# Top-1 mixture of experts after a resampler attention: w2 per turn, shared tiles for the small row groups, five hidden buffers

## The chip, the core and the metric

The kernel runs on one core of one Trainium2 chip. All data is float32. The metric is the device time of one execution in microseconds; the time of a kernel is the median of its runs. TensorE (PE in the profile) multiplies, VectorE (DVE) and ScalarE (ACT) compute elementwise, GpSimd (POOL) computes a little and issues indirect DMAs, SyncE (SP) issues the other DMAs. Each engine runs its instructions in the order in which they are written.

## What is computed

Two stages over 16 sequences of 128 tokens, 256 wide. The first is a resampler attention with 16 heads of 64 and a residual; the change does not touch it. The second is a layer norm and a feed-forward layer with one shared expert and 8 routed experts, of which each token takes one:

```python
scores_aE = x_aD @ router_DE
vals_aK, idx_aK = jax.lax.top_k(scores_aE, 1)
masked_aE = jnp.full_like(scores_aE, -jnp.inf).at[jnp.arange(a)[:, None], idx_aK].set(vals_aK)
gates_Ea = jax.nn.sigmoid(masked_aE).T
routed_in_EaD = gates_Ea[:, :, None] * x_aD[None, :, :]
mid_EaF = silu(einsum('ead,edf->eaf', routed_in_EaD, w1_eDF)) * einsum('ead,edf->eaf', routed_in_EaD, w3_eDF)
routed_out_EaD = einsum('eaf,efd->ead', mid_EaF, w2_eFD)
shared_aD = silu(x_aD @ ws1_DF) * (x_aD @ ws3_DF) @ ws2_FD
out_aD = shared_aD + routed_out_EaD.sum(axis=0)
```

There are 2048 tokens, D = 256, F = 704, 8 experts. The layer adds its result to its input.

## The kernel before

The order of the instructions on all five engines is written out by hand (`manual_schedule`). The attention runs first, eight pairs of sequences after one another, with chunks of the shared expert (`shared_unit`) put between. When its memory is released, at about 520 us, the second stage has the rest of the span.

**Routing** (`route`, L997). Each token has a place among those of its expert. The experts are sorted by their number of tokens, and expert number w in that order gets window w, of 320, 288, 288, 288, 256, 256, 256 and 256 slots (`WINDOWS`). The first 256 slots of window w are tiles 2w and 2w + 1 of 128 rows. What a window has beyond 256, its `REST` (64, 32, 32, 32), is a small tile with the number 16 + w. The number of the slot is worked out by DVE from `win` (the window) and `place` with some twenty small operations (L1098 to L1121, `beyond` at L1106), then `slot_table` (L954) turns it into a table with the token of each slot, with sixteen products `slots` on TensorE (L983). Chunks of the shared expert are put between these by a generator (`yield`). A branch at the end (`overflow`) handles experts that outgrow their window; it is not taken here.

**Weights.** `load_experts` (L920) loads w2 of all 8 experts, in the experts' own order, into one tile `wds`, from the moment that the attention's memory is free. `load_up` (L1236) loads w1 and w3 of one window's expert into one of three tiles `w13`; the first three are issued when the order of the experts is known, and that of window w + 2 in window w. All are issued by SP.

**Inputs.** `gather` (L1188) fetches a tile's rows of `h_rows` by the table, with an indirect DMA of POOL; `gate` (L1201) multiplies them by the gates on DVE. For window 0 TensorE transposes them (`transpose_inputs`, L1207) and DVE copies them to `inputs_t`. For later windows DVE transposes blocks of 32 (`turn_inputs`, L1214), SP writes them to DRAM, and `fetch_inputs` (L1228) reads them back in the right place. `inputs_t` has two tiles, taken in turns.

**Windows.** `up` (L1243) computes chunk f of the hidden layer: four products (two for the half chunk f = 5) on TensorE into a pair of PSUM banks of `ps_s` (two pairs, taken in turns), silu on ACT, the product `mid` on DVE. `out_rows` (L1276) multiplies a tile of `mid`, six products, by w2 into a PSUM bank of `ps_m` (three, in turns), DVE adds the rows of the residual and the shared expert (`sg`, gathered by `stream_rows`, L1264), and POOL scatters the sum to `out`. The expert's number addresses `wds` from a register of TensorE (`value_load`, L1320). A float32 product is two records of the trace. The loop (L1319) goes over the windows:

```python
        for f in range(NF):
            up(w13s[w % 3], inputs_t[w % 2], WINDOWS[w], mids[w % 2], f, f"w{w}")
            if f == 0:
                sgs = [stream_rows(t, rows_of(t)) for t in tiles_of(w - 1)] if w else []
```

After chunk 0 of window w come, in this order: the gathers of `sg` for window w - 1, `turn_inputs(w + 1)`, the gathers for window w + 2, `down_window(w - 1)` with its two or three tiles, `fetch_inputs(w + 1)` and `load_up` for window w + 2. Then chunks 1 to 5. So TensorE's order is chunk 0 of window w, the tiles yr of window w - 1, chunks 1 to 5 of window w. There are two `mids`. `sg` has three buffers (the tag `xr`), gathered rows three (`xg`).

## Time and profile before

| | us |
|---|---|
| median of 3 runs | 748.63 (748.04 to 748.77) |
| profiled execution | 748.45 |
| its span, first to last instruction | 746.6 |
| TensorE busy | 736.0 |
| yr of one window with a small tile, windows 0 to 3 | 8.05 to 8.08 |
| yr of one window without, windows 4 to 7 | 5.34 |
| first products of the experts (chunk 0 of window 0) | from 584.11 |
| first yr tile | from 603.32 |
| SP's loads of w2 issued | 522.88 to 538.4 |
| SP's first loads of w1 and w3 issued | from 542.30 |

The page gives the share of time in which each engine was busy, the same in 40 slices, and the chain of work that ended last, followed back from the last instruction. The timeline lists instructions in the order of time: start, length, engine, line of the code, operation, output and inputs, and in brackets how long the engine stood idle before and what it waited for. A DMA that POOL issues is shown with the time POOL takes to issue it (about 1 us), not with that of the transfer.

### The profile page before, as it was taken

The page shows a single profiled execution, that of the slowest core. Times are in us where ns is not written, and L with a number is a line of the kernel's source. Part 1 is how long each engine was busy: PE and PEld are TensorE (multiplying, and loading weights), DVE is VectorE, ACT ScalarE, POOL GpSimd, SP SyncE. Part 2 cuts the span into 40 slices and gives each one's busy share as a digit, 9 for nine tenths or more (in the row PEclk, how much of TensorE's full clock was granted, in tenths as well). Part 3 has the DMA queues.
Part 4 walks back from the last instruction along what each step waited for, and adds up shares of the span by engine and source line. Part 5 has one row for each costly group of instructions (what it writes and reads, how often), then busy time and mean ns, then how long its engine had stood idle before and what let it go on. Part 6 is the DMA issues. An engine that isn't in the chain of part 4 may idle for free.

```text
span 746.6 us, 11560 instructions
## 1 busy us (share of the span) xinstructions
PE 736.0 (99%) x4096; PEld 572.5 (77%) x4096; DVE 385.8 (52%) x949; ACT 259.1 (35%) x787; POOL 314.4 (42%) x366
## 2 busy tenths in 40 slices
PE   8999999999999999999999999999999999999997
PEld 6857768777677677687686788688888877778886
DVE  5566558558647656665656437634643333333321
ACT  2444534444354354344444554611311011111111
POOL 1363554464355445534643654440104334444220
PEclk9999999999999999999999999999999999999999
DMA  8075735844953953864664634651991345645301
GB/s 297 17 250 195 204 128 179 235 165 154 270 170 127 264 200 129 218 223 143 193 197 137 203 124 165 208 183 56 306 322 55 83 110 154 173 138 162 97 27 46
DMA packets 140773, 125.20 MB, mean 168 GB/s; under 512 B 62484, under 2 KB 124631, under 8 KB 140708
## 3 DMA queue, kind: packets, MB, share of 16 engines
q1 hardware_dynamic: 134356, 108.49, 46.8%
q0 software_dynamic: 4336, 12.46, 5.4%
q10 hardware_dynamic: 2016, 3.43, 1.3%
q8 instruction: 35, 0.57, 0.3%
q14 instruction: 30, 0.25, 0.1%
HBM read 75.49 MB, written 49.02 MB: 167 GB/s over the span
## 4 chain that ended last, share of the span: by engine, by line
PE 93%; DVE 4%; ACT 2%; issue 0%; DMA 0%; ACTq 0%
PE pk L446 15%; PE pv L465 14%; PE u_w L1249 11%; PE S L498 8%; PE O L563 8%; PE p L162 8%; PE pw L579 7%; PE pq L431 7%; PE yr L1279 7%; PE ys L192 5%; ACT pe L517 1%; PE pr L634 1%; PE pr L162 1%; PE ys L245 1%; PE slots L983 0%
## 5 line engine op out<-in xcount | busy, mean ns | idle before, releaser
L530 POOL TENSOR_SCALAR pe<-pe,rs 128x256 f32<-128x256 f32 x256 | 232.5, 926 | 243.7 <-DVE rs L527 243.7
L517 ACT ACTIVATE pe<-S,nmx 128x256 f32<-128x256 f32 x256 | 118.7, 489 | 132.0 <-DVE nmx L510 132.0
L465 PE MATMUL pv<-wv,kvT 128*128 128x512 f32 x256 | 116.5, 599 | 0.2 <-ACT kT L454 0.2
L446 PE MATMUL pk<-kvT,wk 128*128 128x256 f32 x512 | 115.2, 383 | 1.3 <-ACT kT L454 0.7
L446 PEld LDWEIGHTS pk<-kvT,wk 128*128 128x128 f32 x512 | 95.8, 190 | 19.4 <-DVE px L539 2.0
L539 DVE STREAM_TRANSPOSE px<-pe 128x512 f32<-128x512 f32 x128 | 81.4, 682 | 32.0 <-POOL pe L530 32.0
L465 PEld LDWEIGHTS pv<-wv,kvT 128*128 128x128 f32 x256 | 47.2, 190 | 53.2 <-issue 50.6
L1249 PE MATMUL u_w<-xT,w 128*128 128x256 f32 (+2 forms) x352 | 85.6, 399 | 0.3
L1249 PEld LDWEIGHTS u_w<-xT,w 128*128 128x128 f32 x352 | 66.0, 190 | 18.8 <-DVE mid_w L1258 3.3
L510 DVE TENSOR_REDUCE nmx<-S 128x4 f32<-128x1024 f32 x64 | 75.1, 1213 | 9.7 <-PE S L498 9.5
L162 PE MATMUL p<-hT,ws 128*128 128x256 f32 x320 | 73.8, 382 | 0.2 <-DVE mid L178 0.2
L162 PEld LDWEIGHTS p<-hT,ws 128*128 128x128 f32 x320 | 59.9, 190 | 10.0 <-issue 1.3
L563 PEld LDWEIGHTS O<-pT,v 128*64 128x64 f32 x1024 | 55.2, 137 | 14.7 <-issue 12.9
L498 PE MATMUL S<-kT,qT 64*128 64x256 f32 x512 | 63.9, 389 | 0.0
L563 PE MATMUL O<-pT,v 128*64 128x128 f32 x1024 | 63.0, 276 | 0.0
L472 ACT COPY v<-pv 128x512 f32<-128x512 f32 x64 | 38.2, 599 | 63.1 <-PE pv L465 63.1
L527 DVE RECIPROCAL rs<-sums 128x4 f32<-128x4 f32 x64 | 11.4, 177 | 93.4 <-ACT pe L517 93.4
L579 PEld LDWEIGHTS pw<-wo,oT 128*128 128x128 f32 x256 | 48.6, 190 | 12.2 <-issue 3.1
L579 PE MATMUL pw<-wo,oT 128*128 128x256 f32 x256 | 57.9, 379 | 0.0
L431 PE MATMUL pq<-kvT,wq 128*128 128x256 f32 x256 | 57.7, 379 | 0.0
L1257 ACT ACTIVATE rsl_w<-u_w 128x256 f32<-128x256 f32 (+2 forms) x40 | 16.0, 400 | 118.8 <-PE u_w L1249 118.8
L517 ACT ACTIVATION_READ_ACCUMULATOR pe<-S,nmx 128x1 f32 x256 | 56.6, 221 | 0.0
(212 smaller groups left out, 748.5 us busy)
## 6 DMA issues: line engine op xcount, KB each, us to landing
p_blocks<-px SPq DMA_DIRECT2D x64, 512.0 KB, 3.2
pT<-p_blocks SPq DMA_DIRECT2D x64, 512.0 KB, 4.2
w<-in_w_dram SPq DMA_DIRECT2D x8, 704.0 KB, 6.3
wds<-in_w_dram SPq DMA_DIRECT2D x8, 640.0 KB, 8.3
w<-in_w_dram SPq DMA_DIRECT2D x8, 640.0 KB, 5.6
t_blocks<-tx SPq DMA_DIRECT2D x12, 256.0 KB, 2.4
kvT<-t_blocks SPq DMA_DIRECT2D x12, 256.0 KB, 6.2
h_rows<-h SPq DMA_DIRECT2D x8, 256.0 KB, 3.1
```

What stands on the lines that cost most here:

```text
L162: nc.tensor.matmul(ps, lhsT=shared["w13"][:, c, ds(col, P)], rhs=hT[:, c, ts(t, TB)], start=(c == 0), stop=(c == DC - 1),)
L431: nc.tensor.matmul(pq[:, jj], lhsT=wq[:, c, ts(2 * j + jj, P)], rhs=kvTs[g][:, c, :, 1, :], start=(c == 0), stop=(c == DC - 1),)
L446: nc.tensor.matmul(pk[:, jj, :], lhsT=wk[:, c, ts(2 * j + jj, P)], rhs=kvTs[b // 2][:, c, b % 2].rearrange("p t s -> p (t s)"), start=(c = ...
L465: nc.tensor.matmul(pv, lhsT=kvTs[b // 2][:, c, b % 2, t, :], rhs=wv[:, c, ts(n, 512)], start=(c == 0), stop=(c == DC - 1),)
L498: nc.tensor.matmul(pl[:, r, j, :], lhsT=qTs[b // 2][rows, k, b % 2, :], rhs=kTs[b][rows, k, :], start=True, stop=True,)
L510: nc.vector.tensor_reduce(nmx, pl, AX.X, ALU.max, negate=True)
L517: nc.scalar.activation(pes[u][:, h, :], pl[:, r, j, :], AF.Exp, bias=nmx[:, r, j : j + 1], accum_out=sums[u][:, h : h + 1],)
L530: nc.gpsimd.tensor_scalar(w, w, rs[:, i : i + 1], None, ALU.mult)
L539: nc.vector.transpose(px[:, :, t].rearrange("p j h q -> p h j q"), pes[u][:, ts(n, 4), ts(t, S)].rearrange("p h (j k) -> p h j k", k=BL),)
L563: nc.tensor.matmul(o[r * HD : (r + 1) * HD, j, :], lhsT=vs[b][:, t, ts(2 * (4 * half + j) + r, HD)], rhs=pTs[u][:, j // 2, :, t, 2 * (j % ...
L579: nc.tensor.matmul(pw, lhsT=outT[2 * b + k // 4][:, k % 4, :], rhs=wo[:, k, :], start=(k == 0), stop=(k == NP - 1))
L1249: nc.tensor.matmul(ps[:, k, 0:n], lhsT=w13[:, c, ds(col, P)], rhs=xT[:, c, 0:n], start=(c == 0), stop=(c == DC - 1),)
```

## The change

w2 is loaded per window (`load_down`) into five tiles `w2s`, in the order of the windows: those of windows 0 to 4 when the order of the experts is known, between and after the first three `load_up`, and that of window w + 1 in window w for w = 4, 5 and 6. `load_experts` and the expert's register of TensorE go.

The small row groups get common tiles: those of windows 0, 1 and 2 are the rows 0 to 63, 64 to 95 and 96 to 127 of tile 16, that of window 3 is the rows 0 to 31 of tile 17, so there are 18 tiles and not 20. Their slots are numbered by `steps`. Tiles 16 and 17 are gathered, gated and transposed by TensorE together with tiles 0 and 1, and DVE copies their columns to four tiles `inputs_t`; `turn_inputs` and `fetch_inputs` move 256 rows for every window. Their rows of `mid` stay where they are, in five `mids` and not two, until `down_rests` after `down_window(3)` in window 4. It multiplies tile 16 with three products for each f, one for each expert, whose outputs are different partitions of one PSUM bank and so use different columns of the array, and then tile 17 with one for each f. Each of the two tiles gathers its `sg` there, ahead of its products and behind the scatters of tiles 6 and 7.

The half chunk f = 5 takes a bank of `ps_m` and not a pair of `ps_s`.

The diff, without the overflow branch (it follows the new signatures) and empty lines:

```diff
     NREST = sum(r > 0 for r in REST)
-    NTILE = 2 * E + NREST
+    NTILE = 2 * E - (-sum(REST) // P)
     NOVER = -(-(NT - WMAX) // P)
...
-    wds = wexp.tile([P, E, NF, D], F32, name="wds")
     w13s = [wexp.tile([P, DC, 2 * F], F32, name=f"w13_{k}") for k in range(3)]
-    def load_experts():
-        for e in range(E):
-            nc.sync.dma_start(
-                out=wds[:, e, 0:FC, :],
-                in_=w2[e, 0 : FC * P, :].rearrange("(c p) d -> p c d", p=P),
-            )
-            nc.sync.dma_start(out=wds[:, e, FC, :], in_=w2[e, F - P : F, :])
+    w2s = [wexp.tile([P, NF, D], F32, name=f"w2_{k}") for k in range(5)]
     routing = {}
...
         yield "chain"
+        def steps(w, length, name, marks):
+            o = None
+            for k, n, op in marks:
+                for _ in range(n // BL):
+                    a = mscratch.tile([P, length], F32, name=f"{name}{k}_{op.name}", tag=name, bufs=2)
+                    if o is None:
+                        nc.vector.tensor_scalar(a, w, float(k), None, op)
+                    else:
+                        nc.vector.scalar_tensor_tensor(a, w, float(k), o, op, ALU.add)
+                    o = a
+            return o
         slot = mscratch.tile([P, B], F32, name="slot")
         nc.vector.scalar_tensor_tensor(slot, win, 2.0 * P, place, ALU.mult, ALU.add)
+        ahead = steps(win, B, "ahead", [(k + 1, REST[k], ALU.is_ge) for k in range(NREST - 1)])
         shift = mscratch.tile([P, B], F32, name="shift")
         nc.vector.tensor_scalar(
-            shift, win, -float(P), float((2 * E - 2) * P), ALU.mult, ALU.add
-        )
+            shift, ahead, float(BL), float((2 * E - 2) * P), ALU.mult, ALU.add
+        )
+        nc.vector.scalar_tensor_tensor(shift, win, -2.0 * P, shift, ALU.mult, ALU.add)
         nc.vector.scalar_tensor_tensor(shift, place, 2.0 * P, shift, ALU.is_ge, ALU.mult)
         nc.vector.tensor_tensor(slot, slot, shift, ALU.add)
-        def beyond(n, w, length, name, pool):
-            o = pool.tile([P, length], F32, name=name)
-            for k in range(E):
-                step = REST[k] - (REST[k + 1] if k + 1 < E else 0)
-                if step:
-                    less = mscratch.tile([P, length], F32, tag="less", name=f"{name}{k}")
-                    nc.vector.tensor_scalar(less, w, float(k + 1), float(step), ALU.is_lt, ALU.mult)
-                    nc.vector.tensor_tensor(o, n, less, ALU.subtract)
-                    n = o
+        def beyond(n, w, length, name):
+            marks = [(k + 1, REST[k] - (REST[k + 1] if k + 1 < E else 0), ALU.is_lt) for k in range(E)]
+            o = mconst.tile([P, length], F32, name=name)
+            more = steps(w, length, name + "_more", marks)
+            nc.vector.scalar_tensor_tensor(o, more, -float(BL), n, ALU.mult, ALU.add)
             return o
-        over = beyond(place, win, B, "over", mconst)
+        over = beyond(place, win, B, "over")
         away = mscratch.tile([P, B], F32, name="away")
...
                 nc.vector.tensor_copy(expert_i, expert)
-                for w in range(3):
-                    load_up(w, w)
+                load_up(0, 0)
+                load_down(0, 0)
+                load_up(1, 1)
+                load_down(1, 1)
+                load_up(2, 2)
+                for w in range(2, 5):
+                    load_down(w, w)
             if n == 1:
-                load = beyond(total, window, E, "load", mconst)
+                load = beyond(total, window, E, "load")
                 most = mscratch.tile([P, 1], F32, name="most")
...
         )
-        for t in tiles_of(0):
-            gather(t)
+        first = [2 * E, 0, 1] + list(range(2 * E + 1, NTILE))
+        for t in first:
+            gather(t, "xg" if t in first[:3] else "xp")
         for _ in range(4):
             yield
-        for t in tiles_of(0):
+        for t in first:
             gate(t)
         yield
-        for i, t in enumerate(tiles_of(0)):
-            transpose_inputs(t, inputs_t[0][:, :, ds(i * P, rows_of(t))], rows_of(t))
-        for t in tiles_of(1):
+        for t in first[:3]:
+            transpose_inputs(t)
+        for t in (2, 3):
             gather(t)
-    xgs, ups = {}, {}
-    inputs_t = [rwork.tile([P, DC, WMAX], F32, name=f"xT_{k}", bufs=1) for k in range(2)]
-    x_blocks = tc.dram_tile([DC, WMAX // BL, BL, NB, BL], F32, name="x_blocks")
-    def tiles_of(w):
-        return [2 * w, 2 * w + 1] + ([2 * E + w] if REST[w] else [])
-    def rows_of(t):
-        return P if t < 2 * E else REST[t - 2 * E]
-    def gather(t, n=None):
-        n = n or rows_of(t)
-        xg = rwork.tile([P, D], F32, tag="xg", name=f"xg_{t}")
+        yield
+        for t in first[3:]:
+            transpose_inputs(t)
+    xgs = {}
+    inputs_t = [rwork.tile([P, DC, WMAX], F32, name=f"xT_{k}", bufs=1) for k in range(NREST)]
+    x_blocks = tc.dram_tile([DC, 2 * NB, BL, NB, BL], F32, name="x_blocks")
+    rests = [[] for _ in range(NTILE - 2 * E)]
+    for w in range(NREST):
+        at = sum(REST[:w])
+        assert at // P == (at + REST[w] - 1) // P
+        rests[at // P].append((w, at % P, REST[w]))
+    def gather(t, tag="xg"):
+        xg = rwork.tile([P, D], F32, tag=tag, name=f"xg_{t}")
         nc.gpsimd.indirect_dma_start(
-            out=xg[0:n, :],
+            out=xg,
             out_offset=None,
             in_=h_rows,
-            in_offset=Offset(ap=routing["table"][0:n, t : t + 1], axis=0),
+            in_offset=Offset(ap=routing["table"][:, t : t + 1], axis=0),
             bounds_check=NT,
...
         xgs[t] = xg
-    def gate(t, n=None):
-        n = n or rows_of(t)
-        nc.vector.tensor_scalar(
-            xgs[t][0:n, :], xgs[t][0:n, :], routing["gates"][0:n, t : t + 1], None, ALU.mult
-        )
-    def transpose_inputs(t, xT, n):
+    def gate(t):
+        nc.vector.tensor_scalar(xgs[t], xgs[t], routing["gates"][:, t : t + 1], None, ALU.mult)
+    def transpose_inputs(t, to=None):
         xg = xgs.pop(t)
-        px = ps_m.tile([P, DC, n], F32, tag="mm", name=f"px_{t}")
+        px = ps_m.tile([P, DC, P], F32, tag="mm", name=f"px_{t}")
         for c in range(DC):
-            nc.tensor.transpose(px[:, c, :], xg[0:n, ts(c, P)], ident[0:n, 0:n])
-        nc.vector.tensor_copy(xT, px)
+            nc.tensor.transpose(px[:, c, :], xg[:, ts(c, P)], ident)
+        if to is None and t < 2 * E:
+            to = inputs_t[t // 2][:, :, ts(t % 2, P)]
+        if to is not None:
+            nc.vector.tensor_copy(to, px)
+            return
+        for w, at, n in rests[t - 2 * E]:
+            nc.vector.tensor_copy(inputs_t[w][:, :, ds(2 * P, n)], px[:, :, ds(at, n)])
     def turn_inputs(w):
-        for i, t in enumerate(tiles_of(w)):
-            n = rows_of(t)
+        for i in range(2):
+            t = 2 * w + i
             gate(t)
             px = rwork.tile([P, DC, NB, BL], F32, tag="xp", name=f"xp_{t}")
-            nc.vector.transpose(
-                px[0:n], xgs.pop(t)[0:n, :].rearrange("p (c k j) -> p c j k", c=DC, k=BL)
+            nc.vector.transpose(px, xgs.pop(t).rearrange("p (c k j) -> p c j k", c=DC, k=BL))
+            nc.sync.dma_start(
+                out=x_blocks[:, ts(i, NB)].rearrange("c i k j q -> (i k) c (j q)"),
+                in_=px.rearrange("p c j q -> p c (j q)"),
             )
-            nc.sync.dma_start(
-                out=x_blocks[:, ds(i * NB, n // BL)].rearrange("c i k j q -> (i k) c (j q)"),
-                in_=px[0:n].rearrange("p c j q -> p c (j q)"),
-            )
     def fetch_inputs(w):
-        n = WINDOWS[w]
         for c in range(DC):
             nc.sync.dma_start(
-                out=inputs_t[w % 2][:, c, 0:n].rearrange("p (i q) -> p i q", q=BL),
-                in_=x_blocks[c, 0 : n // BL].rearrange("i k j q -> (k j) i q"),
+                out=inputs_t[w % NREST][:, c, 0 : 2 * P].rearrange("p (i q) -> p i q", q=BL),
+                in_=x_blocks[c].rearrange("i k j q -> (k j) i q"),
             )
+    def expert_of(w):
+        return nc.sync.value_load(routing["expert"][0:1, w : w + 1], min_val=0, max_val=E - 1)
     def load_up(k, w):
-        e = nc.sync.value_load(routing["expert"][0:1, w : w + 1], min_val=0, max_val=E - 1)
+        e = expert_of(w)
         a1, a3 = (a[ds(e, 1)].rearrange("e (c p) f -> p (e c) f", p=P) for a in (w1, w3))
...
         nc.sync.dma_start(out=w13s[k][:, :, F + FR : 2 * F], in_=a3[:, :, 0 : FC * P])
+    def load_down(k, w):
+        e = expert_of(w)
+        a2 = w2[ds(e, 1)]
+        nc.sync.dma_start(
+            out=w2s[k][:, 0:FC, :],
+            in_=a2[:, 0 : FC * P, :].rearrange("e (c p) d -> p (e c) d", p=P),
+        )
+        nc.sync.dma_start(
+            out=w2s[k][:, FC, :], in_=a2[:, F - P : F, :].rearrange("e p d -> p (e d)")
+        )
     def up(w13, xT, n, mid, f, name):
-        ps = ps_s.tile([P, 2, 512], F32, tag="S", name=f"u_{name}_{f}")
+        if f < FC:
+            ps = ps_s.tile([P, 2, 512], F32, tag="S", name=f"u_{name}_{f}")
+        else:
+            ps = ps_m.tile([P, 1, 512], F32, tag="mm", name=f"ur_{name}")
         sl = mwork.tile([P, WMAX], F32, tag="sl", name=f"rsl_{name}_{f}")[:, 0:n]
...
             nc.vector.tensor_tensor(mid[hi, FC, 0:n], ps[hi, 0, 0:n], sl[hi, :], ALU.mult)
-    def stream_rows(t, n, table=None):
+    def stream_rows(t):
         sg = mwork.tile([P, D], F32, tag="xr", name=f"sg_{t}", bufs=3)
         nc.gpsimd.indirect_dma_start(
-            out=sg[0:n, :],
+            out=sg,
             out_offset=None,
             in_=s_rows,
-            in_offset=Offset(ap=routing["table"][0:n, t : t + 1], axis=0),
+            in_offset=Offset(ap=routing["table"][:, t : t + 1], axis=0),
             bounds_check=NT,
...
         return sg
-    def out_rows(t, n, e, mid, sg):
+    def out_rows(t, parts, sg):
         py = ps_m.tile([P, D], F32, tag="mm", name=f"yr_{t}")
+        n = max(r.stop for r, _, _ in parts)
         for f in range(NF):
-            nc.tensor.matmul(
-                py[0:n, :],
-                lhsT=mid[:, f, 0:n],
-                rhs=wds[:, ds(e, 1), f, :].rearrange("p e d -> p (e d)"),
-                start=(f == 0),
-                stop=(f == NF - 1),
-            )
+            for rows, mid, wd in parts:
+                nc.tensor.matmul(
+                    py[rows, :], lhsT=mid[:, f, :], rhs=wd[:, f, :], start=(f == 0), stop=(f == NF - 1)
+                )
         nc.vector.tensor_tensor(sg[0:n, :], py[0:n, :], sg[0:n, :], ALU.add)
...
         )
-    load_experts()
     aside = route()
...
     hidden_t = ctx.enter_context(tc.tile_pool(name="hidden_t", bufs=1))
-    mids = [hidden_t.tile([P, NF, WMAX], F32, name=f"mid_w{k}") for k in range(2)]
+    mids = [hidden_t.tile([P, NF, WMAX], F32, name=f"mid_w{k}") for k in range(5)]
     for mid in mids:
...
     def down_window(w, sgs):
-        for i, (t, sg) in enumerate(zip(tiles_of(w), sgs)):
-            out_rows(t, rows_of(t), ups[w], mids[w % 2][:, :, ds(i * P, rows_of(t))], sg)
+        for i in range(2):
+            out_rows(2 * w + i, [(slice(0, P), mids[w % 5][:, :, ts(i, P)], w2s[w % 5])], sgs[i])
+    def down_rests():
+        for k, parts in enumerate(rests):
+            t = 2 * E + k
+            out_rows(
+                t,
+                [
+                    (slice(at, at + n), mids[w][:, :, ds(2 * P, n)], w2s[w])
+                    for w, at, n in parts
+                ],
+                stream_rows(t),
+            )
     for w in range(E):
-        ups[w] = nc.tensor.value_load(
-            routing["expert"][0:1, w : w + 1], min_val=0, max_val=E - 1
-        )
         for f in range(NF):
-            up(w13s[w % 3], inputs_t[w % 2], WINDOWS[w], mids[w % 2], f, f"w{w}")
+            up(w13s[w % 3], inputs_t[w % NREST], WINDOWS[w], mids[w % 5], f, f"w{w}")
             if f == 0:
-                sgs = [stream_rows(t, rows_of(t)) for t in tiles_of(w - 1)] if w else []
+                sgs = [stream_rows(2 * w - 2 + i) for i in range(2)] if w else []
                 if w + 1 < E:
...
                 if w + 2 < E:
-                    for t in tiles_of(w + 2):
-                        gather(t)
+                    gather(2 * w + 4)
+                    gather(2 * w + 5)
                 if w:
...
                     shared_unit()
+                if w == NREST:
+                    down_rests()
                 if w + 1 < E:
...
                     load_up((w + 2) % 3, w + 2)
+                if NREST <= w < E - 1:
+                    load_down((w + 1) % 5, w + 1)
...
```

More of the change, by code (lines that the diff above doesn't have):

```diff
@@ L1339, in resampler_attn__then__top1_moe_kernel @@
                     load_up((w + 2) % 3, w + 2)
+                if NREST <= w < E - 1:
+                    load_down((w + 1) % 5, w + 1)
     def ending():
-        rest = held(mids[E % 2][:, :, 0:TB])
-        sgs = [stream_rows(t, rows_of(t)) for t in tiles_of(E - 1)]
+        rest = held(mids[E % 5][:, :, 0:TB])
+        sgs = [stream_rows(2 * E - 2 + i) for i in range(2)]
         next(rest)
@@ L1349, in overflow @@
     def overflow():
-        area = mids[E % 2].rearrange("p f t -> p (f t)")
+        area = mids[E % 5].rearrange("p f t -> p (f t)")
         used = [0]
@@ L1407, in overflow @@
         routing.update(late)
-        mid = mids[E % 2]
+        mid = mids[E % 5]
         nc.gpsimd.memset(mid[0 : P - FR, FC, :], 0.0)
         for t in range(NOVER):
-            gather(t, P)
-            gate(t, P)
+            gather(t)
+            gate(t)
             xT = inputs_t[0][:, :, 0:P]
-            transpose_inputs(t, xT, P)
-            e = nc.tensor.value_load(routing["expert"][0:1, t : t + 1], min_val=0, max_val=E - 1)
-            sg = stream_rows(t, P)
+            transpose_inputs(t, xT)
+            sg = stream_rows(t)
             load_up(0, t)
+            load_down(0, t)
             for f in range(NF):
                 up(w13s[0], xT, P, mid, f, f"o{t}")
-            out_rows(t, P, e, mid[:, :, 0:P], sg)
+            out_rows(t, [(slice(0, P), mid[:, :, 0:P], w2s[0])], sg)
         routing.update(kept)
```

## The prediction

> **What bounds the kernel now.** I read the page's busy shares first, then the slices, the chain that ended last, TensorE's timeline of the expert stage, the chain of that stage, and last the timelines of POOL and SP.
>
> ```profile
> PE 736.0 (99%) x4096; PEld 572.5 (77%) x4096; DVE 385.8 (52%) x949; ACT 259.1 (35%) x787; POOL 314.4 (42%) x366
> PE   8999999999999999999999999999999999999997
> PEclk9999999999999999999999999999999999999999
> PE 93%; DVE 4%; ACT 2%; issue 0%; DMA 0%; ACTq 0%
> ...
> 544.29 0.64 PE L983 MATMUL slots<-sent,at_row 128*128 128x40 f32 x4 [0.84 <-DVE at_row L976]
> ...
> 641.43 8.05 PE L1279 MATMUL yr<-wds,mid_w 128*128 x36
> 678.18 5.34 PE L1279 MATMUL yr<-wds,mid_w 128*128 x24
> ...
> 683.52 6.92 PE u_w L1249 x32
> 690.45 0.02 issue
> 690.47 0.39 ACT rsl_w L1257
> 690.88 0.43 DVE mid_w L1258
> 691.36 1.99 PE u_w L1249 x8
> 693.36 5.18 PE yr L1279 x24
> ...
> 664.14 1.03 POOL L1288 DMA_INDIRECT out_dram<-sg,table  x1 [0.31 <-issue]
> 667.52 0.99 POOL L1288 DMA_INDIRECT out_dram<-sg,table  x1 [2.35 <-DMA out_dram<-sg,table]
> 672.44 0.89 POOL L1288 DMA_INDIRECT out_dram<-sg,table  x1 [3.92 <-DMA out_dram<-sg,table]
> ...
> 668.11 0.38 SPq L1239 DMA_DIRECT2D w<-in_w_dram  x1
> ```
>
> TensorE is the bound, at an undiminished clock: time is won only by giving it fewer columns to stream or fewer gaps. A full yr tile (6 products, 12 records) takes 5.18/2 = 2.59 us, 0.216 us a record. A window with a small tile has 36 records instead of 24, though that tile fills only 32 or 64 columns of the array. At 690.45 the chain leaves TensorE for ACT and DVE: the next window's first product waits for a PSUM pair of `ps_s`. At 544.29 TensorE waits for DVE's routing arithmetic. POOL's lines show that each scatter to `out` waits until the one before has landed, and that this took longer (667.52 to 672.44) once SP had issued the next expert's weights (668.11).
>
> **What the Trainium skill says.** "TensorEngine Tiling (Array Packing)", Key Properties: tiles work independently, but changing the tiling mode drains TensorE. The trace agrees with both halves: the attention products O on two 64-column halves start in pairs 6 ns apart, and from a 128-column product to a 32- or 64-column one the step is 309 ns, not 216. "TensorE: Matmul & The Clock Gate", Measured speedup vs the span model, has three column tiles at 2.38 times one; no row here mixes 64 and 32 columns. The same page's Part 1 has the clock halve after an idle window of about 3.4 us; this trace has no such gap. "DMA: Bandwidth & Descriptors", Queues, rings and completion order: each DMA engine takes turns between the queues. Here an `xr` load of POOL took 7.0 us to land while SP's queue was full (DMA share 1.06, 544 to 556) and 3.2 us at 570.
>
> **The change, part by part.** The profiled execution took 748.45 us (span 746.6 and 1.85 around it), the median is 748.63; the sum is made on the former, and 0.2 goes on at the end.
>
> 1. *Small tiles of windows 0 to 2 are no longer multiplied in their windows.* Each costs 12 x 0.216 + 2 switches of 0.093 = 2.78 us; three of them, -8.4 us. The fourth moves into the next item.
>
> 2. *down_rests at window 4.* Tile 16 has 3 x 12 = 36 records on columns 0-63, 64-95 and 96-127; tile 17 has 12 on 32 columns. Tile 16 costs 2.7 us if all three run at once, 7.8 us if none do; if 64 and 32 count as different modes, six times (2 x 0.216 + 0.093) x 2 = 6.3 us. I take 6.3, since the page on tiling lists them as separate configurations. Tile 17 is 2.7 us. But TensorE does not decide here. The residual rows of tiles 16 and 17 are gathered inside down_rests, behind scatters on POOL's in-order queue. Counted from the first yr record of window 3 (660.26 in the old trace):
>  - the first scatter at 3.4 (its DVE addition ends at 663.60), the second when that has landed, 3.38 later as in 664.14 to 667.52: 6.8;
>  - gather 16 at 8.1 (1.0 of POOL and its 0.3 between issues). Gathers land 2.8 us after issue (median; 2.0 to 6.2). SP's loads fill the queue then (DMA share 0.95 from 667.4 to 674.1), and the scatter of 667.52 needed 4.92 instead of 3.38, so I add 1.5: 12.4. DVE adds by 12.9;
>  - scatter 16 from 12.95, gather 17 at 14.3. `load_down(5)` lengthens SP's 1.7 MB of that window to 2.5 MB; at the 274 GB/s of that stretch it ends about 676.5, 16.2 on this scale. With 1.2 us for that, gather 17 lands at 18.3, DVE's addition ends at 18.8.
>  DVE is in order: behind that addition stands the product `mid` of chunk 1 of window 4, and the third chunk's matmuls wait for its `ps_s` buffer. TensorE can reach them at 17.9 (5.2 + 0.1 + 6.3 + 2.7 + 0.1 + 16 x 0.216), but gets them at 19.2 (18.8 + 0.42). In the old trace they start at 671.70, 11.4. So +7.8 us.
>
> 3. *The half chunk f = 5 moves to `ps_m`.* At seven window ends its single records step by 0.45 (or 0.43) us instead of 0.216 (0.243); over the seven that is 1.4 us, caused by the wait at 690.45. After the change the next chunk takes the buffer of chunk 3, free since 1.7 us: -1.4 us. The `ps_m` buffer it takes was emptied a window earlier. Next in line is nothing that I can find.
>
> 4. *Routing arithmetic.* `shift` gains five small DVE operations, `over` loses one, at 0.19 us each (0.10 for the one that depends on no neighbour): +0.75. `load` loses one (-0.2), three operations over 18 instead of 20 tiles lose 0.03 each (-0.1). DVE runs without a gap from 533.97 to at_row, and TensorE waits at its end, so all counts: +0.45 us.
>
> 5. *Transposes of the inputs.* One more full tile, two records of 0.11: +0.2. Tile 16's eviction becomes three copies instead of one, and the matmul p after it waits for that buffer (576.24 now): +0.2. Together +0.4 us.
>
> 6. *w2 loaded after the routing.* Nothing is loaded from 523 to 541; from 542 on SP has 4.3 MB of w1 and w3 and 3.9 MB of w2. At 370 GB/s (SP's queue moved that from 544 to 553) this is 22 us, with POOL's transfers over at about 568. The first gathers, issued from 563.7, may land 3 us late, at 571 to 573; their gates run at 574.04, so about 1 us of cover is left. Each w2 is there 15 us before its yr. Cost 0; if the cover is gone, TensorE waits at 574.8 by as much. The later loads (one a window, 0.79 MB) stand behind `load_up` on SP, and the next SP instruction is a window away.
>
> 7. *Cost nothing:* PE's register operations (0.055 us each, beside matmuls of 0.216), two gathers and two scatters fewer and three memsets more (0.35 us each) on POOL, fewer DVE transposes in windows 1 to 3.
>
> Sum: -8.4 + 7.8 - 1.4 + 0.45 + 0.4 = -1.15 us. 748.45 - 1.15 + 0.2 = **747.4 us**.
>
> **Rivals.**
> - *A, the forecast:* the late gather takes back most of what the small tiles give. For it: POOL waited for landed scatters nine times, 30.5 us in all, in the expert stage. It hardly depends on whether the columns run at once: even with no concurrency at all chunk 3 would start at about 19.4. 746.5 to 748.4.
> - *B, gathers land in time:* both at 2.8 us, scatters at 3.38. Then gather 16 lands at 10.9; it and the second scatter's landing at 10.2 let scatter 16 go at 11.4 and gather 17 at 12.7, landed at 15.5, chunk 3 at 16.4 where the columns run at once: 2.8 us better, 744.6. Against it: the DMA share of 0.95. I take 744.6 to 746.5.
> - *C, the clock drops:* if the columns run at once, TensorE is done with chunk 2 at 14.2 and idle for 5.0 us. By the page on the clock gate the clock may then halve, at an estimated 1.7 to 3.4 us for the window in which it recovers: 749.1 to 750.8. Against it: with a switch of mode at every turn TensorE is busy until 17.9.
> - *D, slower:* in down_rests, two gathers at 7.0 us as `xr` had with a full queue. Gather 16 lands at 15.1, scatter 16 goes at 15.6, gather 17 at 16.9, landed at 23.9, chunk 3 at 24.8, 5.6 us later than in A: 753.0. It decides against the old kernel once the two landings together take 1.2 us more than the 8.3 I gave them. For it: SP's queue then holds 2.5 MB, not 1.7. Against: of all 20 gathers of `sg`, with weights loading in most windows, the median was 2.8.
>
> **How the numbers follow.** A 0.50, B 0.22, C 0.13, D 0.15. Runs agree to 0.1%, and 0.2%, 1.5 us, is what can be told from no change. Faster than 747.1: B and a quarter of A, 0.34. Slower than 750.1: most of D and some of C, 0.20. Within: 0.46. The range leaves out the lowest part of B and the worse half of D: 745.0 to 751.5. A's own is 746.5 to 748.4.
>
> **What would show it.** In the new trace: no yr record of under 128 columns before window 4; at window 4 POOL's scatter, gather, scatter, gather in that order, the last gather some 14 us after the first yr; DVE's second addition of down_rests waiting for a DMA, TensorE idle by 1 us (columns by turns) to 5 us (at once) before chunk 3; start steps of the 64- and 32-column records telling which; no gap at window ends; a wait of about 1.3 us at the first slots product. Wrong if the gathers are not what DVE waits for, if a gap opens at the first transposes (w2 loads), or if PEclk falls in that slice.

## The result, and the profile after

| | before | after |
|---|---|---|
| median | 748.71 us (748.04 to 751.01, 13 runs) | 750.86 us (749.87 to 752.33, 13 runs) |
| profiled execution | 748.45 us | 750.86 us |
| its span | 746.6 us | 749.1 us |
| first yr of window 0 | 603.32 | 604.42 |
| first yr of window 3 | 660.26 | 651.76 |
| first yr of window 4 | 678.18 | 680.73 |
| last products ys begin | 735.83 | 737.71 |

The changed kernel is slower: ratio 1.0029, 95% interval 1.0020 to 1.0038. The prediction was 747.4 us, faster. The range, 745.0 to 751.5, holds the median; the sign is wrong.

The table of stages says where. At the first yr of window 3 the changed kernel is 8.5 us ahead. At the first yr of window 4 it is 2.55 us behind: one window gave back 11 us. That window holds `down_rests`. From the page of the changed kernel, the busy times, two rows of the slices and the chain's shares:

```profile
PE 734.9 (98%) x4098; PEld 573.0 (76%) x4098; DVE 383.3 (51%) x948; ACT 259.5 (35%) x787; POOL 309.9 (41%) x363
...
PE   8999999999999999999999999999999999989996
...
PEclk9999999999999999999999999999999999999999
...
PE 9%; DMA 1%; issue 1%; DVE 0%; POOL 0%; POOLq 0%; DVEq 0%
```

One new dent in TensorE's row, at the slice from 655 to 674, and a chain that no longer runs through TensorE to the start: followed back from the end, it leaves TensorE at 673 us for DVE, and DVE for a gather of POOL. (The shares are small because it breaks off at 655 us.) PEclk shows nothing: a dip of 3 us is lost in a slice of 18.7. The timeline of TensorE there:

```profile
651.76 14.30 PE L1310 MATMUL yr<-w,mid_w 128*128 128x256 f32 x72
665.99 3.72 PE L1277 MATMUL u_w<-xT,w 128*128 128x256 f32 x16
673.05 5.26 PE L1277 MATMUL u_w<-xT,w 128*128 128x256 f32 x16 [3.34 <-DVE mid_w L1286]
```

Two things are lost. Chunks 3 and 4 of window 4 (16 records) begin 3.5 us after TensorE is free for them (3.34 in the bracket, which counts from the end of the record before), waiting for a product `mid` of DVE. And they take 5.26 us, where chunks 1 and 2, the same work, took 3.72. DVE in that stretch, with the two additions of `down_rests` in the middle:

```profile
657.14 0.42 DVE L1313 TENSOR_TENSOR sg<-yr,sg 128x256 f32<-128x256 f32 x1 [2.17 <-PE yr L1310]
666.51 0.42 DVE L1313 TENSOR_TENSOR sg<-yr,sg 128x256 f32<-128x256 f32 x1 [8.95 <-DMA sg<-s_rows,table]
672.25 0.41 DVE L1313 TENSOR_TENSOR sg<-yr,sg 32x256 f32<-32x256 f32 x1 [5.32 <-DMA sg<-s_rows,table]
672.59 0.73 DVE L1286 TENSOR_TENSOR mid_w<-u_w,rsl_w 128x256 f32<-128x256 f32 x2
```

DVE stands still twice, 9 and 5 us, each time until a gather of `sg` has landed; `mid` of chunks 1 and 2, in one line at 672.59, come behind. POOL, which issues those gathers (L1294) and the scatters (L1315), and SP with the loads of weights:

```profile
658.60 1.01 POOL L1315 DMA_INDIRECT out_dram<-sg,table  x1 [2.27 <-issue]
659.91 1.04 POOL L1294 DMA_INDIRECT sg<-s_rows,table  x1 [0.30 <-issue]
667.21 1.00 POOL L1315 DMA_INDIRECT out_dram<-sg,table  x1 [6.26 <-DVE sg L1313]
668.52 1.03 POOL L1294 DMA_INDIRECT sg<-s_rows,table  x1 [0.30 <-issue]
```

```profile
659.07 0.38 SPq L1253 DMA_DIRECT2D w<-in_w_dram  x1
659.65 0.38 SPq L1254 DMA_DIRECT2D w<-in_w_dram  x1
660.21 0.37 SPq L1255 DMA_DIRECT2D w<-in_w_dram  x1
662.24 0.37 SPq L1260 DMA_DIRECT2D w<-in_w_dram  x1
```

The gather of tile 16 is issued at 659.91 and DVE gets it at 666.5: SP's 1.4 MB of w1 and w3 start at the same time, and behind them the 0.8 MB of w2 (L1260). The packets of the scatter of 658.60 begin to move only at 662.33, those of gather 16 at 664.18. The addition ends, scatter 16 goes at 667.21, and only then is gather 17 issued, as the order in the program wants it. The table of windows has, for each stretch, its length, PE, PEld, DVE, ACT and POOL busy, the granted clock, the DMA share and GB/s:

```profile
658.00:662.00 4.00, 4.00 (x24) 1.20 (x20) 0.00 (x0) 0.00 (x0) 2.05 (x2) 1.00 0.80 155
662.00:666.00 4.00, 4.00 (x24) 1.60 (x23) 0.00 (x0) 0.00 (x0) 0.00 (x0) 1.00 1.04 384
669.50:673.00 3.50, 0.21 (x1) 0.00 (x0) 0.75 (x3) 0.38 (x1) 0.05 (x1) 0.97 0.17 37
673.00:676.00 3.00, 2.95 (x7) 2.42 (x8) 0.32 (x1) 0.00 (x0) 2.37 (x3) 0.50 0.04 8
```

The DMA engines are busy for 0.80 of the time up to 662 and full (1.04) up to 666. From 673 on the granted clock is 0.50: six records start 0.427 us after one another and not 0.216, after TensorE had stood idle. The 0.97 of the stretch before says that the clock fell about 0.2 us ahead of the first of these records, so while TensorE was still waiting.

So the theory, T: the gathers behind the scatters on POOL hold DVE, DVE's order holds `mid` and through it TensorE (3.5 us), and the idleness then halves the clock (about 1.5 us). The rivals: the traffic alone, wherever the gathers stand; PSUM rather than DVE's order; a slow pace that has nothing to do with idleness.

### The profile page after: what moved, and what is told of

Same layout as the page of the kernel before. It is cut to its first block, busy times and chain, and to the rows that moved or that the text cites. A ratio compares the mean times of both kernels' runs of the same rounds, so it can differ in the third digit from the quotient of the medians.

```text
span 749.1 us, 11455 instructions
## 1 busy us (share of the span) xinstructions
PE 734.9 (98%) x4098; PEld 573.0 (76%) x4098; DVE 383.3 (51%) x948; ACT 259.5 (35%) x787; POOL 309.9 (41%) x363
## 5 line engine op out<-in xcount | busy, mean ns | idle before, releaser
L1277 PE MATMUL u_w<-xT,w 128*128 128x256 f32 (+2 forms) x320 | 78.9, 402 | 3.3 <-DVE mid_w L1286 3.3
L1277 PEld LDWEIGHTS u_w<-xT,w 128*128 128x128 f32 x320 | 61.7, 194 | 17.8 <-DVE mid_w L1286 3.7
L527 DVE RECIPROCAL rs<-sums 128x4 f32<-128x4 f32 x64 | 11.4, 177 | 93.7 <-ACT pe L517 93.7
L579 PEld LDWEIGHTS pw<-wo,oT 128*128 128x128 f32 x256 | 48.6, 190 | 12.2 <-issue 3.1
```

What stands on the lines that cost most here:

```text
L579: nc.tensor.matmul(pw, lhsT=outT[2 * b + k // 4][:, k % 4, :], rhs=wo[:, k, :], start=(k == 0), stop=(k == NP - 1))
L1277: nc.tensor.matmul(ps[:, k, 0:n], lhsT=w13[:, c, ds(col, P)], rhs=xT[:, c, 0:n], start=(c == 0), stop=(c == DC - 1),)
```

## The experiments

Of each kernel below, times on one scale with the others are counted from its own first yr of window 3.

**early_gathers.** Both gathers at the head of window 4, into two buffers of their own:

```diff
...
                 sgs = [stream_rows(2 * w - 2 + i) for i in range(2)] if w else []
+                if w == NREST:
+                    rest_sgs = [stream_rows(2 * E + k) for k in range(len(rests))]
...
-                stream_rows(t),
+                rest_sgs[k],
```

> The changed kernel, with the sg rows of tiles 16 and 17 gathered at the head of window 4, next to those of tiles 6 and 7, into two buffers of their own. In the changed kernel chunk 3 of window 4 starts 21.3 us after the first yr of window 3, 3.5 us after TensorE is free for it, and its eight records then take 1.7 us more than at 0.216 a record. Theory T (the gathers behind the scatters on POOL hold DVE, and through it TensorE): chunk 3 starts at 17.8, no record above 0.31 us after it, 3.5 + 1.3 = 4.8 us less than the changed kernel: about 746.0, ratio to the kernel before 0.9965. Rival R1 (what holds DVE is the traffic of that stretch, not where the gathers stand on POOL): the gathers or scatters land late wherever they stand, chunk 3 starts later than at 20, the ratio stays at 1.002 or more.

Measured: 746.16 us, ratio 0.9964 (0.9950 to 0.9977), 4.7 us less than the changed kernel. TensorE and DVE of this kernel:

```profile
652.17 14.30 PE L1313 MATMUL yr<-w,mid_w 128*128 128x256 f32 x72
666.40 7.17 PE L1277 MATMUL u_w<-xT,w 128*128 128x256 f32 x32
```

```profile
664.35 0.42 DVE L1316 TENSOR_TENSOR sg<-yr,sg 128x256 f32<-128x256 f32 x1 [6.37 <-PE yr L1313]
666.51 0.41 DVE L1316 TENSOR_TENSOR sg<-yr,sg 32x256 f32<-32x256 f32 x1 [1.73 <-PE yr L1313]
```

Chunks 1 to 4 are one group of 32 records without a gap, and the additions wait for TensorE, no longer for a DMA. The loads run as before (2.5 MB from 658.7 to 668.8), so traffic alone (R1) costs TensorE nothing. T holds.

**late_addition.** All DMAs and their order as in the changed kernel up to the wait; only tile 17's addition and scatter go behind `mid` of chunk 3:

```diff
...
-        nc.vector.tensor_tensor(sg[0:n, :], py[0:n, :], sg[0:n, :], ALU.add)
+        if late is not None:
+            late.append((t, n, py, sg))
+        else:
+            finish_rows(t, n, py, sg)
...
+            if f == 3 and late:
+                finish_rows(*late.pop())
```

> The changed kernel, with only tile 17's addition (and its scatter) moved on DVE and POOL behind the products mid of chunk 3 of window 4; all gathers, loads and scatters ahead of it stay where they are. Theory T, its DVE part (mid of chunk 1 stands behind the addition of tile 17 in DVE's order): the addition of tile 16 still ends at about 15.2 us after the first yr of window 3, mid of chunk 1 at 15.5, chunk 3 starts at 17.8 when TensorE is free, no slow records: 4.8 us less than the changed kernel, 746.0, ratio 0.9965. Rival R2 (chunk 3 waits for PSUM or for inputs, not for DVE's order): it still starts at about 21, ratio 1.003.

Measured: 746.37 us, ratio 0.9971 (0.9959 to 0.9984). DVE:

```profile
668.31 0.42 DVE L1319 TENSOR_TENSOR sg<-yr,sg 128x256 f32<-128x256 f32 x1 [10.01 <-DMA sg<-s_rows,table]
669.17 0.42 DVE L1286 TENSOR_TENSOR mid_w<-u_w,rsl_w 128x256 f32<-128x256 f32 x1 [0.44 <-ACT rsl_w L1285]
...
674.05 0.41 DVE L1319 TENSOR_TENSOR sg<-yr,sg 32x256 f32<-32x256 f32 x1 [1.00 <-DMA sg<-s_rows,table]
```

Gather 16 is even later than in the changed kernel (its addition starts 15.8 after the first yr of window 3, against 14.75), gather 17 is not in before 674, and TensorE has no gap. What cost the time was one 32-row addition ahead of `mid` in an in-order engine. R2 is out.

**loads_held.** SP copies eight numbers of tile 17's sum to DRAM ahead of the loads of window 4 (`last` is tile 17's `sg`):

```diff
...
+                if w == NREST:
+                    nc.sync.dma_start(out=gone, in_=last[0:1, 0:8])
                 if 1 <= w < E - 2:
                     load_up((w + 2) % 3, w + 2)
```

> The changed kernel, where in window 4 SP copies eight numbers of tile 17's sum to DRAM before it issues load_up(6) and load_down(5), so that these 2.5 MB start only when tile 17 is added. POOL's and DVE's order is untouched. Theory T2 (the long landings of scatter 7, 5.4 us, and of gather 16, 6.1 us, come from SP's loads in the same DMA engines): they land in about 3.4 and 2.8 us, gather 17 in 2.8, its addition ends at about 16.5 after the first yr of window 3, chunk 3 starts at 17.8, no slow records: 4.8 us less than the changed kernel, 746.0, ratio 0.9965. Rival R3 (the landings are long because the indirect DMAs queue behind one another): landings as now, chunk 3 at 21, ratio 1.003.

Measured: 747.02 us, ratio 0.9982 (0.9975 to 0.9989): 3.8 us less than the changed kernel, 1.0 short of the 4.8. DVE, then TensorE:

```profile
664.15 0.42 DVE L1313 TENSOR_TENSOR sg<-yr,sg 128x256 f32<-128x256 f32 x1 [6.38 <-PE yr L1310]
669.91 0.41 DVE L1313 TENSOR_TENSOR sg<-yr,sg 32x256 f32<-32x256 f32 x1 [5.34 <-PE u_w L1277]
```

```profile
670.71 3.72 PE L1277 MATMUL u_w<-xT,w 128*128 128x256 f32 x16 [0.80 <-DVE mid_w L1286]
```

Gather 16 now lands before its product is done: the addition starts at 12.2 (TensorE decides), not 14.75. T2 holds, R3 is out: at least 2.5 us of gather 16's landing were SP's loads. With early_gathers this means that the full wait takes both, the place behind the scatters on POOL and SP's loads at that moment. The missing 1.0 us is a wait of that length that stays before chunk 3: gather 17 is issued at 14.2, behind scatter 16, and needs 3.75 us to its addition, not the 2.8 that I expected (the bracket of the second line names TensorE, but the gather had landed only just before, at 669.8). The clock stays at full speed in the profiled execution. Four of the 21 runs took 748.8 to 749.5 us, with a mean clock of 0.996 where the other 17 have 0.997 to 1.0; in these the wait probably grew long again.

**w2_load_held.** The same small copy one line further down, so that only `load_down(5)` waits.

> The changed kernel, where in window 4 only load_down(5), 0.8 MB, waits for tile 17's sum (the small copy of loads_held ahead of it); load_up(6), 1.7 MB, goes as in the changed kernel. In the changed kernel the addition of tile 16 starts 14.75 us after the first yr of window 3, with both held 12.2 (where TensorE's product ends). Theory U (the 0.8 MB that the change added there are what makes gather 16 late): addition at 12.2, chunk 3 of window 4 at 18.7, about 747.0, ratio 0.998. Rival V (load_up(6), which the kernel before has at the same place, is enough): addition at 14.3 to 14.75, chunk 3 at 20.8 to 21.3, ratio 1.002 to 1.003.

Measured: 751.72 us, ratio 1.0031 (1.0013 to 1.0049), and the addition of tile 16 at 14.75, as in the changed kernel. Rival V: the w1 and w3 loads, which the old kernel has at the same place, are enough; the w2 that the change added does nothing to the landing here. Chunk 3 starts at 21.3, after 3.5 us of idleness, as in the changed kernel too, but the granted clock goes to 0.50 already 2.5 us into the wait (1.00 from 669.3 to 671.6, 0.50 from 671.7 to 678.4) and stays there for 6.8 us, not 3.4: twelve steps of 0.427 us and not six.

**filled_wait, partly_filled_wait, three_products_in_wait.** Extra products on TensorE inside the wait, seven, two and three of them:

```diff
+            if w == NREST and f == 3:
+                fill = ps_m.tile([P, D], F32, tag="mm", name="fill")
+                for _ in range(7):
+                    nc.tensor.matmul(
+                        fill, lhsT=ident, rhs=inputs_t[0][:, 0, 0:D], start=True, stop=True
+                    )
             up(w13s[w % 3], inputs_t[w % NREST], WINDOWS[w], mids[w % 5], f, f"w{w}")
```

> The changed kernel, with seven extra products of the identity with the inputs (14 records, 3.0 us, result unused) on TensorE between chunks 2 and 3 of window 4, inside its wait of 3.5 us. Theory C (the slow records after the wait, 0.427 us instead of 0.216, come from TensorE having stood idle): the wait ends where it ended, 21.3 us after the first yr of window 3, but all records of chunk 3 take 0.216 us: 1.3 to 1.7 us less than the changed kernel, about 749.4, ratio 1.001. Rival R4 (something else halves the pace then, such as the DMA load): the slow records stay, ratio 1.003.

> The changed kernel, with two extra products (4 records, 0.86 us, result unused) right behind chunk 2 of window 4, so that TensorE stands idle for 2.6 us and not 3.5 before chunk 3. Theory W (there is a length of idleness between 1.0 and 3.5 us below which the pace doesn't fall, and 2.6 is below it): records of chunk 3 at 0.216, about 749.4, ratio 1.001. Rival X (2.6 us is enough, or the drop follows from the mean over a longer stretch): records of 0.427 after the wait, for 2 us or more, ratio 1.002 to 1.003.

> The changed kernel, with three extra products (6 records, 1.3 us, result unused) right behind chunk 2 of window 4. The wait before chunk 3 began to vary from run to run with the landing of gather 16 (addition of tile 16 at 14.4 to 15.8 us after the first yr of window 3), so TensorE should stand idle for 1.9 to 3.3 us. In the last run, with two products, it stood idle for 3.9 us and the pace fell; at 1.0 us it did not. Theory W (an idle time below some 3.4 us leaves the pace alone): records of chunk 3 at 0.216. Rival X (less is enough): records of 0.427 after it, for 2 us or more. If the idle time comes out above 3.4 us the run tells nothing.

Measured with seven: 749.30 us, ratio 1.0010 (1.0004 to 1.0017), 1.6 us less than the changed kernel. TensorE:

```profile
669.24 3.19 PE L1362 MATMUL fill<-xT,ident 128*128 128x256 f32 x14
672.53 3.72 PE L1277 MATMUL u_w<-xT,w 128*128 128x256 f32 x16
```

More work on the bounding engine made the kernel faster: chunk 3 starts where it did, 21.1, and its 16 records take 3.72 us again. Theory C holds. With two products the experiment missed its aim: gather 16 came 1 us later in that execution (addition at 15.8), TensorE stood idle for 3.9 us and not 2.6, the records of 0.427 were there, and the ratio, 1.0022 (0.9998 to 1.0046), decides nothing. With three (one run, 748.48 us) TensorE was idle for 1.6 us and no record was slow. So waits of up to 1.6 us left the pace alone here and those of 3.5 us and more did not; w2_load_held shows that 2.5 us of idleness can be enough for the clock to fall.

**four_columns_alone, early_four_columns.** The 64 rows of window 0 as two products of 32 rows:

```diff
-                    (slice(at, at + n), mids[w][:, :, ds(2 * P, n)], w2s[w])
+                    (slice(at + b, at + b + BL), mids[w][:, :, ds(2 * P + b, BL)], w2s[w])
                     for w, at, n in parts
+                    for b in range(0, n, BL)
```

> The changed kernel with tile 16 as four products of 32 columns, the gathers left where they were. Theory T with S: TensorE has tile 16 done 4.1 us sooner and waits that much longer; chunk 3 of window 4 still starts at about 21.3 us after the first yr of window 3 and is followed by slow records, as in the changed kernel: 750.9, ratio 1.003. Rival R6 (TensorE's time for tile 16 is on the path to chunk 3): up to 4.1 us less, ratio 0.9975.

> early_gathers, with the 64 rows of window 0 in tile 16 multiplied as two products of 32 rows, so that each step has four products of 32 columns and no change between 64 and 32. In the changed kernel tile 16 takes 6.7 us: six steps of 1.13, the 64-column product alone and only the two 32-column ones at once. Theory S (a change of mode keeps the products apart; products of one mode on different columns run at once): 12 steps of 0.216, 2.6 us, so 4.1 us less than early_gathers (746.2): about 742.1, ratio to the kernel before 0.991. Rival R5 (only two run at once, or the bank of PSUM or the weight loads limit it): 24 steps of 0.216, 5.2 us, 1.5 us less: 744.7, ratio 0.9946.

Measured alone: 751.56 us, ratio 1.0037 (1.0025 to 1.0049). On top of early_gathers: 742.19 us, ratio 0.9914 (0.9901 to 0.9928). TensorE of the first, then of the second:

```profile
652.13 10.64 PE L1310 MATMUL yr<-w,mid_w 128*128 128x256 f32 x84
662.70 3.72 PE L1277 MATMUL u_w<-xT,w 128*128 128x256 f32 x16
672.88 6.14 PE L1277 MATMUL u_w<-xT,w 128*128 128x256 f32 x16 [6.46 <-DVE mid_w L1286]
```

```profile
651.45 10.64 PE L1313 MATMUL yr<-w,mid_w 128*128 128x256 f32 x84
662.02 7.17 PE L1277 MATMUL u_w<-xT,w 128*128 128x256 f32 x32
```

The group of yr records falls from 14.30 to 10.64 us although it has 12 records more. The records of the four products start 6 or 7 ns apart, the next four 0.22 us later: all four run at once. The same edit is worth 4.0 us of the median where the gathers are early and nothing where they are late: there it turns into idleness (6.6 us instead of 3.5), and the half clock lasts longer (16 records in 6.14 us, not 5.26). That the longer idleness made it last longer is not shown: in w2_load_held it lasts as long, 6.8 us, after 3.5 us.

**early_four_split.** Also tile 17's six products on three column groups, two on each, with three additions on DVE:

```diff
...
+                for f in range(2):
+                    for g in range(3):
+                        nc.tensor.matmul(
+                            py[ds(g * BL, BL), :],
+                            lhsT=mids[r][:, 2 * g + f, ds(2 * P, n)],
+                            rhs=w2s[r][:, 2 * g + f, :],
...
```

> early_four_columns, with tile 17's six products on three groups of 32 columns, two of them on each group (sums of f = 0 and 1, 2 and 3, 4 and 5), which DVE adds with three additions and not one. Theory S: 4 steps of 0.216 and not 12, 1.7 us less; DVE's two further additions, 0.8 us, end before mid of chunk 1 is wanted by chunk 3: 740.5, ratio to the kernel before 0.989. Rival Y (DVE's additions delay mid of chunk 1 and with it chunk 3): 741.2 or more, ratio 0.990 or above.

Measured: 740.83 us, ratio 0.9890 (0.9874 to 0.9907), faster than both kernels by 8 to 10 us. TensorE, tiles 6, 7 and 16, then tile 17:

```profile
651.93 8.07 PE L1313 MATMUL yr<-w,mid_w 128*128 128x256 f32 x72
659.81 1.04 PE L1360 MATMUL yr<-w,mid_w 128*32 128x256 f32 x12
660.78 7.17 PE L1277 MATMUL u_w<-xT,w 128*128 128x256 f32 x32
```

No gap follows: DVE's further additions are not in the way.

**half_chunk_alone, w2_by_turns_alone.** The kernel before with one part of the change each:

```diff
-        ps = ps_s.tile([P, 2, 512], F32, tag="S", name=f"u_{name}_{f}")
+        if f < FC:
+            ps = ps_s.tile([P, 2, 512], F32, tag="S", name=f"u_{name}_{f}")
+        else:
+            ps = ps_m.tile([P, 1, 512], F32, tag="mm", name=f"ur_{name}")
```

> The kernel before, with only the half chunk f = 5 in a bank of ps_m. The prediction's step: 1.4 us less, 747.3, ratio 0.998. From the two traces (each window ends 0.25 to 0.43 us sooner, 2.5 us over eight): 2.4 us less, 746.3, ratio 0.9967. Rival R7 (the bank of ps_m it takes makes yr or the shared chunks wait): no gain, ratio 1.000.

> The kernel before, with only w2 loaded per window into five tiles, in the order and at the places of the changed kernel; small tiles, routing and the half chunk as before. The prediction's step: 0 (ratio 1.000); in particular no wait at the first transposes (574.8) beyond the two gaps of before. Rival R8 (the loads after the routing, or the later ones beside the gathers, cost): the first gathers land late or the scatters and gathers of windows 4 to 6 do, by up to 1 us, ratio 1.0013.

Measured: 746.49 us, ratio 0.9970 (0.9957 to 0.9982), for the half chunk; 748.51 us, 0.9997 (0.9989 to 1.0006), for w2. The half chunk gains 2.1 us, not 1.4, and needs nothing else of the change. w2 costs nothing, and the two gaps at the first transposes are as before.

## Why the prediction was wrong, step by step

| step | predicted | measured | from |
|---|---|---|---|
| 1, small tiles out of the windows | -8.4 | -8.7 | first yr of window 0 to that of window 3, without the half chunk |
| 2, `down_rests` in window 4 | +7.8 | +11.4 | first yr of window 3 to that of window 4, without the half chunk |
| 3, half chunk | -1.4 | -2.1 | half_chunk_alone against before, seven window ends |
| 4, routing | +0.45 | +0.5 | up to the first slots product, 10.50 to 11.04 from the chunk at 534 |
| 5, transposes | +0.4 | +0.5 | from the first transpose to chunk 0 of window 0, 9.30 to 9.83 |
| 6, 7 | 0 | 0 | w2_by_turns_alone; no new gap |
| end of the program | not in the sum | +0.6 | last addition to the end, 5.4 to 6.0 |
| sum | -1.15 | +2.2 | |

The two traces differ by 2.5 us in span; the 0.3 us missing from the sum are in the attention, which is the same in both kernels. The medians differ by 2.15. Step 2 alone missed by 3.6; the other misses, -0.3, -0.7, +0.6 and two of about 0.1, nearly cancel, which is luck.

**What was right.** The forecast named the bottleneck, the order of POOL and the engine that it holds. Its times for `down_rests` can be checked one by one, after the first yr of window 3: first scatter 3.4 predicted and 3.5 measured; second 6.8 and 6.8; gather 16 issued 8.1 and 8.15; then it ends. Tile 16 by turns of mode was right as well: 6.7 us against 6.3.

**The step that failed** is one term of step 2, the landing of gather 16: "Gathers land 2.8 us after issue (median; 2.0 to 6.2) [...] so I add 1.5: 12.4". The addition that waits for it started at 14.75, 6.6 us after the issue and not 4.3. All that follows kept the predicted distances: scatter 16 at 15.45, gather 17 at 16.8, its addition at 20.5 (3.7 us after the issue; predicted 4.0), chunk 3 at 21.3 instead of 19.2. That is 2.1 of the 3.6 us by which step 2 missed. In loads_held, where the loads start later, the same gather lands 2.9 us after its issue, in the changed kernel 6.5: SP's loads add 3.6 us and not the 1.5 of the forecast.

The old trace had the right number. From it, the times to landing of all DMAs of the tile `sg`, and POOL's timeline in window 6:

```profile
DMA to landing us min/median/max: 2.0/2.8/6.2
```

```profile
686.93 1.04 POOL L1266 DMA_INDIRECT sg<-s_rows,table  x1 [0.30 <-issue]
688.28 1.01 POOL L1266 DMA_INDIRECT sg<-s_rows,table  x1 [0.30 <-issue]
```

SP's queue (the inputs of the next window, then w1 and w3) moved its bytes from 611.5 to 618.6, 629.5 to 638.8, 647.7 to 654.9, 667.4 to 674.1 and 685.6 to 692.4. Of the twenty gathers of `sg`, only these two were issued well inside such a stretch; their packets had ended by 692.97, 6.0 and 4.7 us after the issue (nobody waited for them: DVE's additions came at 696). All others were issued where the queue was empty or almost so, because POOL reached them late. The median of 2.8 described the empty queue; the question was about the full one, and the answer was near the maximum of 6.2, which is the gather of 686.93. In the changed kernel, where more gathers are issued into the loads, their median is 5.1 and nine of the 18 took 5.7 to 7.5. The same holds for the scatter: the forecast's 1.5 us is from the one of 667.52, with 4.92 us to the next instead of 3.38, but after those at 612.92, 632.58 and 650.38 it was 6.7, 6.3 and 6.0 to the next. w2_load_held shows that the old loads suffice, so nothing of the change was needed to see it.

**The second loss, 1.5 us,** is rival C's clock, set aside because "with a switch of mode at every turn TensorE is busy until 17.9". That was right, but the idle time of the forecast, 1.3 us, became 3.5 with the later landing. "TensorE: Matmul & The Clock Gate", Part 1, of the Trainium skill says that the clock halves after an idle window of about 3.4 us and that this window runs on its own, not from the start of the idleness. The waits agree: no fall after 1.0 and 1.6 us, a fall after 3.5, 3.9 and 6.6. The granted clocks agree with the second half: the half clock begins 2.5 us (w2_load_held), 3.2 (the changed kernel), 3.9 (partly_filled_wait) and 4.7 us (four_columns_alone) after TensorE has run out of work, so not at one distance, and lasts 3.4 or 6.8 us, once or twice the same length. With a whole idle window w2_load_held does not agree: there TensorE was still at work for the first 0.9 of the 3.4 us ahead of the fall. I priced a late gather and a lower clock as separate rivals; they are one case, since the one makes the other. Rival D had the sign turn once the two landings took 9.5 us together; to the additions that waited for them they took 6.6 and 3.7, 10.3. By itself that would have given 748.45 - 1.15 + 2.1 = 749.4 us for the profiled execution, hardly slower; the clock made it plain.

**Step 3** was too small because only the first record after each wait was counted. The second is late as well (0.320 us instead of 0.216): seven times 0.1 is the 0.7 us that was missing. In windows 0 to 2 of the old trace the second record after the small tile is late in the same way (0.346 us instead of 0.243): three times 0.1 is the 0.3 us of step 1. **The end of the program** was not in the sum. In both kernels SP's last instructions are waits and a branch past the overflow code; the branch took 2.9 us after the change and 2.6 before, the waits ahead of it 0.35 more. All kernels built on the changed one have 11.4 to 11.6 us from the last ys to the end, the three without it 10.8 to 11.0. Why was not tried.

The changed kernel's parts are worth more than they cost: without the wait it stands at 746.2, with the columns used fully at 740.8. But the half chunk alone stands at 746.5 (ratios 0.9964 and 0.9970): the common tiles, with what they add to routing and transposes, gain next to nothing until their columns run at once.

## What to carry to other kernels

Before a median latency is used for a moved DMA, look at when the measured ones were issued: take those that met the traffic which the moved one will meet, even if there are only two. Where a small, late operation (here one addition of 32 rows) stands ahead of the bounding engine's next input on an in-order engine, fetch its data a stage earlier or put it behind that input; either is a few lines, and each was worth the whole loss. A stall of TensorE of some 3 us is to be priced with its clock, as one case.

## What was unexpected

- Products of 32 columns on four different column groups start 6 to 7 ns apart and cost what one costs (12 steps of 0.216 us for 48 records); a 64-column product among 32-column ones runs alone, with a step of 309 ns at each change. This agrees with "TensorEngine Tiling (Array Packing)", Key Properties, of the Trainium skill: independent tiles, and a drain at a change of mode.
- How long the half clock lasts does not follow the idle time: 3.4 us after 3.5 and 3.9 us of idleness, 6.8 us after 6.6 but also after 3.5 (w2_load_held). What goes with it in these four executions is how much of the first 3.4 us at half clock TensorE worked: 3.1 us or all of them, and the clock came back; 1.5 or 2.5 us, and it took another 3.4. Four cases do not make a rule.
- The landing of one gather under SP's load varied by 1.7 us between kernels whose instructions up to it are the same (addition of tile 16 at 14.1 to 15.8), enough to carry TensorE's wait across the length at which the clock falls. The 13 runs of the changed kernel spread over 2.5 us, the 5 of early_gathers, which has no such wait, over 0.7. (The kernel before has none either: its 13 runs spread over 1.2 us, but for one at 751.01 that nothing here explains.)
